# A graph layer's second pass: TensorE's results staged by ScalarE two experts ahead of VectorE, with the order fixed on four engines

## The chip, the cores and the metric

The kernel runs on one core of a Trainium2 chip. Its time is the device time of one execution in microseconds; the times of a kernel are given as the median of several runs. Engines are named as in the profile: PE is TensorE (matrix products, with PEld its weight loads), DVE is VectorE, ACT is ScalarE, POOL is GpSimd, which here issues the indirect DMAs, and SP is SyncE.

## The reference

Two graph layers run over 3125 nodes with 256 features and 103125 edges sorted by destination. Only the second one matters here:

```
W   = einsum('rb,bio->rio', comp, basis)              # 8 relations
agg = segment_sum((xn @ W[r])[src, edge_type], dst)   # a sum over each node's edges
h   = layernorm(gelu(agg + xn @ loop_w + h_bias + xn))
x   = x + h + linear_attention(xn)
xn  = layernorm(x) ; logits = xn @ Wr + br            # 8 experts, the best 2 weighted by softmax
x   = x + sum_e w[:, e] * (gelu(xn @ W1[e] + b1[e]) @ W2[e] + b2[e])
```

Everything is float32. The kernel computes all eight experts for every node and multiplies by the weight, which is zero for six of them.

## The kernel before

The nodes lie in 25 tiles of 128, with 128 nodes on the partitions and 256 features behind one another; `x` (3.2 MB in SBUF) holds all tiles. The last tile, 24, is partly filled. The table of `h` is complete at about 1396 us of the profiled execution, and the second pass follows it; until about 1500 us the jobs beside its gathers are those of the attention. The pass has two things to do at once.

**Edges.** For each tile of nodes, the rows of a table of `h` in HBM are gathered, 128 rows at a time, one row for each node of the tile. A gather is one indirect DMA issued by POOL (L193, `gt<-htab_f,idx2g`). The gathers go into a pool of five buffers (`gp1`), each of which takes up to four. When the gathers of one buffer have landed, DVE adds the blocks up: a 128x512 add and a 128x256 add among the blocks (L1356), and a 128x256 add to the sum of the tile (L1361). This is called an add chain here. A buffer is free for POOL again when its chain is through.

**Groups.** The tiles are worked through in groups of 4, 2, 4, 3, 3, 2, 2, 2, 1, 1 and 1 tiles (15 to 18 first, then 23 and 24, then from 19 to 22 downwards). The first group's sums are begun while the table is still being written (L2114 adds those, one instruction for up to four tiles). When the sums of a group are complete, a list of jobs is put on a queue, `bg`, and these jobs are done between the add chains of the next group. After each chain the loop hands out credit, in proportion to the gathers of that chain (0.9 to 1.3 for each, by how much work is queued), and takes jobs off the queue, each with a cost written beside it, until the credit is used up. The jobs of a group of k tiles are:

- `sums_a`, `sums_b`, `sums_c`: the products of `loop_w` and of the attention's part for each tile (`loops`, L2300 to L2302, on PE into PSUM), then two DVE adds that read PSUM (`mg`, L2307, and `x`, L2308) and a Gelu into `hh` (L2309).
- `states_a` to `states_d`: the two layer norms, with square roots on ACT (`root`, L2327).
- `routes_a` and `routes_b`: transposes and logits on PE (L2370, L2378), and the routing weights `wf` on DVE, with an exponent on ACT (L214) in the middle (`top2`).
- `shares`: the transposed weights, and the product with the experts' output biases (`constants`, L2425).
- `step(0)` to `step(9)`: `hidden(e)` does 8 products for an expert (four blocks of 128 hidden features, two halves of the input, L2408) into four PSUM banks, each followed by a Gelu on ACT (L2412) into `hT`. `outputs(e)` does four products a tile into PSUM (L2439), two tiles to a bank, with two banks in turn. `take`, at the start of the next step, is DVE's: one instruction a tile, `x = py * w + x` (L2458), which reads the product in PSUM and `x` in SBUF; the bias's product is added by L2450.

The last four steps of a group are kept back (`late`) and put between the first jobs of the next group. When a group is finished its tiles are put on the list `leaving`, and are scattered to the output (L240, an indirect DMA on POOL) between later gathers; those of tiles below 11 leave after the last gather.

The order of the instructions on DVE and POOL is that of the program (`manual_schedule`); the order on PE and ACT is chosen by a scheduler. All engines run their queues in order and wait for one another by semaphores.

Of the kernel before, what the change touches and what calls it, by code (L numbers as in the profile page):

```python
# [20 lines left out]
P = 128  # L21
# [39 lines left out]
SECONDS = 5  # L61

# [38 lines left out]
def gps_kernel(ctx: ExitStack, tc: tile.TileContext, a, out):  # L101
# [1215 lines left out]

    def fast():
        fx = ExitStack()
# [245 lines left out]
        with ExitStack() as l0x:  # L1565
# [376 lines left out]
            ET = mybir.EngineType  # L1942
# [216 lines left out]
        with ExitStack() as l1x:  # L2159
# [23 lines left out]
            f1 = l1x.enter_context(tc.tile_pool(name="f1", bufs=3))  # L2183
# [57 lines left out]
            def att_ctx(t):  # L2241
                r = rows(t)
                pt = ps_tr.tile([P, 2, P], F32, name="pt")
                PE.transpose(pt[:r, 0, :], kT[:, t * P : t * P + r], ident)
                ks = kp.tile([P, P], F32, name="ks1", bufs=3)
                S.activation(ks[:r, :], pt[:r, 0, :], AF.Copy, scale=rs2[:r, t : t + 1])
                PE.matmul(pctx, ks[:r, :], x[:r, t, :], start=(t == 0), stop=(t == NT - 1))

            def att_sum():
                S.copy(g_t, pctx)  # L2250
# [35 lines left out]
            class Group:  # L2286


                def __init__(self, tiles, accs):
                    self.tiles, self.accs = tiles, accs  # L2290
                    self.k, self.s = len(tiles), slice(tiles[0], tiles[-1] + 1)
                    self.at0, self.n = tiles[0] * P, sum(rows(t) for t in tiles)
                    self.hT, self.ys = {}, []

                def loops(self, a, b):

                    for j in range(a, min(b, self.k)):
                        pa = self.pa[j] = ps_mm.tile([P, 512], F32, name="mm")
                        at = slice(self.tiles[j] * P, (self.tiles[j] + 1) * P)
                        PE.matmul(pa, xT[:, 0, at], w_lu[:, 0, :], start=True, stop=False)  # L2300
                        PE.matmul(pa[:, :D], ones_row, b_h, start=False, stop=False, skip_group_check=True)
                        PE.matmul(pa, xT[:, 1, at], w_lu[:, 1, :], start=False, stop=True)  # L2302

                def gelus(self, a, b):
                    for j in range(a, min(b, self.k)):
                        t, mg, pa = self.tiles[j], self.accs[j], self.pa.pop(j)
                        V.tensor_tensor(mg, mg, pa[:, :D], op=ALU.add)  # L2307
                        V.tensor_tensor(x[:, t, :], x[:, t, :], pa[:, D:], op=ALU.add)  # L2308
                        S.activation(self.hh[:, j, :], mg, AF.Gelu)  # L2309

                def sums_a(self):
                    self.hh = fin.tile([P, 4, D], F32, name="hh")
                    self.mvh = [small.tile([P, 4, 2], F32, name=f"mvh{i}") for i in range(2)]
                    self.rsh = [small.tile([P, 4], F32, name=f"rsh{i}") for i in range(3)]
                    self.pa = {}
                    self.loops(0, 2)

                def sums_b(self):
                    self.gelus(0, 2)
                    self.loops(2, 4)  # L2320

                def sums_c(self):
                    self.gelus(2, 4)
# [41 lines left out]
                def routes_a(self):  # L2365
# [9 lines left out]
                    self.pl = ps_tr.tile([P, 512], F32, name="pt")  # L2375
                    for j, t in enumerate(self.tiles):
                        for c in range(2):
                            PE.matmul(  # L2378
                                self.pl[:, j * NX : (j + 1) * NX], xT[:, c, t * P : (t + 1) * P], wr1[:, c, :],
                                start=(c == 0), stop=(c == 1),  # L2380
                            )

                def routes_b(self):
                    k = self.k
                    lg1 = fin.tile([P, 4, NX], F32, name="lg1")
                    V.tensor_tensor(
                        lg1[:, :k, :], self.pl[:, : k * NX].rearrange("p (j e) -> p j e", e=NX),
                        br1[:, None, :].to_broadcast([P, k, NX]), op=ALU.add,
                    )
                    w_full, _ = top2(lg1[:, :k, :], k, fin)  # L2390
                    V.tensor_copy(wf[:, self.s, :], w_full)

                def shares(self):
# [6 lines left out]
                    self.constants()  # L2400

                def hidden(self, e):
                    n, at0 = self.n, self.at0
                    hT = self.hT[e] = f1.tile([P, FC, 4 * P], F32, name="hT1")
                    for f in range(FC):
                        ph = ps_mm.tile([P, 512], F32, name="mm")
                        for c in range(2):
                            PE.matmul(  # L2408
                                ph[:, :n], w1s[e][:, c, f * P : (f + 1) * P], xT[:, c, at0 : at0 + n],
                                start=(c == 0), stop=(c == 1),  # L2410
                            )
                        S.activation(hT[:, f, :n], ph[:, :n], AF.Gelu, bias=b1[:, e, f : f + 1])  # L2412

                def bank(self):
                    turn[0] += 1
                    return ps_acc.tile([P, 512], F32, name="py", tag=f"acc{1 + turn[0] % 2}")

                def constants(self):

                    for j0 in range(0, self.k, 2):  # L2420
                        pb = self.bank()
                        two = self.tiles[j0 : j0 + 2]
                        for j, t in enumerate(two):
                            r, at = rows(t), (j0 + j) * P
                            PE.matmul(  # L2425
                                pb[:r, j * D : (j + 1) * D], self.wT[:, at : at + r], b2a, start=True, stop=True
                            )
                        self.ys.append((None, two, pb))

                def outputs(self, e):  # L2430

                    hT = self.hT.pop(e)
                    for j0 in range(0, self.k, 2):
                        py = self.bank()
                        two = self.tiles[j0 : j0 + 2]
                        for j, t in enumerate(two):
                            r, at = rows(t), (j0 + j) * P
                            for f in range(FC):
                                PE.matmul(  # L2439
                                    py[:r, j * D : (j + 1) * D], hT[:, f, at : at + r], w2s[e][:, f, :],  # L2440
                                    start=(f == 0), stop=(f == FC - 1),
                                )
                        self.ys.append((e, two, py))

                def take(self):

                    for e, two, py in self.ys:
                        if e is None and rows(two[-1]) == P:
                            d = x[:, two[0] : two[-1] + 1, :].rearrange("p t d -> p (t d)")
                            V.tensor_tensor(d, d, py[:, : len(two) * D], op=ALU.add)  # L2450
                            continue
                        for j, t in enumerate(two):
                            r = rows(t)
                            d, y = x[:r, t, :], py[:r, j * D : (j + 1) * D]
                            if e is None:
                                V.tensor_tensor(d, d, y, op=ALU.add)
                            else:
# [202 lines left out]
```

## Time and profile before

| What | us |
|---|---|
| median of 7 runs | 2478.44 |
| lowest to highest of them | 2476.69 to 2487.56 |
| the profiled execution, its own time | 2480.69 |
| its span | 2478.9 |

| Engine, whole span | busy us | share |
|---|---|---|
| POOL | 1723.6 | 70% |
| PE | 1695.7 | 68% |
| DVE | 1267.0 | 51% |
| ACT | 560.6 | 23% |

A row of instruction groups reads: line, engine, operation, output <- input, shape, count, then busy time in us, the mean of one in ns, and the idle time of the engine just before these instructions with what ended most of it. "issue" means that the engine waited for nothing that the profile shows. In a row of the timeline the first number is the start, the second the duration, and the brackets hold the idle time before it and its releaser. In a table of windows each engine has its busy time and, in parentheses, its instructions.

### The profile page before, as it was taken

What the parts mean: (1) busy time and instruction counts of PE and PEld (TensorE: products, weight loads), DVE (VectorE), ACT (ScalarE), POOL (GpSimd) and SP (SyncE); (2) the same over time, 40 slices, a digit from 0 to 9 for tenths busy, and PEclk for the clock granted to TensorE, in tenths of its full rate; (3) what the DMA queues carried; (4) which work ended last, traced back from release to release, by engine and by line L of the source; (5) the groups of instructions that cost most, each with busy time, mean ns of one, the idle gap of its engine ahead of it and who ended that gap; (6) DMA issues with size and microseconds to landing.
All of it is one profiled execution on the core that took longest, in us unless ns stands there. A gap on an engine that the chain in (4) does not pass through costs nothing.

```text
span 2478.9 us, 20996 instructions
## 1 busy us (share of the span) xinstructions
PE 1695.7 (68%) x6033; PEld 1106.6 (45%) x6033; DVE 1267.0 (51%) x3537; ACT 560.6 (23%) x1275; POOL 1723.6 (70%) x1830
## 2 busy tenths in 40 slices
PE   3446777403926614375799736997889799797987
PEld 2323444202614302243444323665556567575876
DVE  7654556436544545444656335464536365454552
ACT  4222321001201101021322122131213132232333
POOL 4577777777777777777016776777777777777771
PEclk9777887655967766777799967998899899888988
DMA  6544444344344443444146834333333333333330
GB/s 192 141 110 110 108 107 127 105 105 140 103 105 107 107 106 104 107 105 105 61 181 231 289 112 136 103 107 111 98 107 105 105 102 103 103 103 103 102 101 23
DMA packets 125962, 290.09 MB, mean 117 GB/s; under 512 B 41386, under 2 KB 63982, under 8 KB 122632
## 3 DMA queue, kind: packets, MB, share of 16 engines
q0 software_dynamic: 83184, 230.02, 33.9%
q1 hardware_dynamic: 38122, 55.88, 6.6%
q10 hardware_dynamic: 4526, 2.71, 0.4%
q8 instruction: 51, 0.84, 0.1%
q14 instruction: 79, 0.65, 0.1%
HBM read 249.07 MB, written 39.41 MB: 116 GB/s over the span
## 4 chain that ended last, share of the span: by engine, by line
PE 19%; POOL 12%; issue 9%; DVE 5%; DMA 4%; ACT 1%; DVEq 0%; POOLq 0%; ACTq 0%
POOL gt L193 12%; PE mm L2408 6%; PE py L2439 6%; PE mm L188 5%; DMA gt<-htab_f,idx2g 3%; DVE gt L1356 1%; DMA out_dram<-x,id_i 1%; DVE bnst L162 1%; PE pt L2378 1%; DVE acc L1361 0%; DVE x L2458 0%; DMA gt<-htab_f,soon 0%; PE mm L2302 0%; DVE x L2343 0%; PE mm L2300 0%
## 5 line engine op out<-in xcount | busy, mean ns | idle before, releaser
L193 POOL DMA_INDIRECT gt<-btab,idx x814 | 799.9, 983 | 253.1 <-issue 223.6
L193 POOL DMA_INDIRECT gt<-htab_f,idx2g x742 | 731.3, 986 | 236.5 <-issue 200.4
L1356 DVE TENSOR_TENSOR gt<-gt 128x256 f32<-128x256 f32 (+1 forms) x767 | 411.5, 537 | 228.0 <-DMA gt<-htab_f,idx2g 211.6
L2408 PE MATMUL mm<-xT,w 128*128 128x256 f32 (+4 forms) x1408 | 386.9, 429 | 61.6 <-DVE x L2308 59.8
L2439 PE MATMUL py<-w,hT 128*128 128x256 f32 (+1 forms) x1600 | 374.8, 389 | 17.6 <-DVE x L2458 17.4
L2439 PEld LDWEIGHTS py<-w,hT 128*128 128x128 f32 (+1 forms) x1600 | 305.8, 194 | 79.6 <-DVE x L2458 11.2
L2408 PEld LDWEIGHTS mm<-xT,w 128*128 128x128 f32 x1408 | 250.3, 203 | 173.8 <-issue 128.7
L1620 DVE COPY slots<-gt 128x4 f32<-128x4 f32 (+1 forms) x214 | 38.5, 180 | 436.2 <-DMA gt<-btab,idx 436.0
L2412 ACT ACTIVATE hT<-mm,b 128x256 f32<-128x256 f32 (+4 forms) x352 | 170.7, 495 | 377.1 <-PE mm L2408 373.2
L188 PE MATMUL pt<-w_own,xT 128*128 128x256 f32 x100 | 39.5, 531 | 250.3 <-DVE acc L1845 250.3
L188 PE MATMUL mm<-w_rel,xT 128*128 128x512 f32 x400 | 176.1, 598 | 3.0 <-ACT xT L183 2.9
L1361 DVE TENSOR_TENSOR acc<-acc,gt 128x256 f32<-128x256 f32 x371 | 158.5, 427 | 12.7
L2458 DVE SCALAR_TENSOR_TENSOR x<-py,wf,x 128x256 f32<-128x256 f32 x200 | 87.8, 477 | 146.5 <-PE py L2439 146.3
L188 PEld LDWEIGHTS pt<-w_own,xT 128*128 128x128 f32 x100 | 24.3, 268 | 261.3 <-DVE acc L1845 254.8
L188 PEld LDWEIGHTS mm<-w_rel,xT 128*128 128x128 f32 x400 | 75.4, 191 | 96.1 <-issue 84.3
L1503 PE MATMUL mm<-xT,w 128*128 128x384 f32 (+2 forms) x320 | 94.6, 460 | 14.3 <-DMA w<-in_f_W_dram 14.3
L1863 PE MATMUL pmean<-ones,xt 128*128 128x1 f32 (+1 forms) x100 | 21.9, 323 | 119.9 <-DVE xt L171 119.9
L193 POOL DMA_INDIRECT gt<-htab_f,soon x72 | 75.8, 1053 | 39.0 <-issue 18.9
L1852 ACT ACTIVATE rs<-rs 128x3 f32<-128x3 f32 (+2 forms) x11 | 2.2, 203 | 434.6 <-DVE rs L1851 434.6
L1532 PE MATMUL mm<-w,hT 128*128 128x256 f32 x400 | 98.5, 401 | 2.0 <-ACT hT L1524 2.0
L1532 PEld LDWEIGHTS mm<-w,hT 128*128 128x128 f32 x400 | 77.0, 198 | 33.6 <-issue 18.9
L188 PE MATMUL mm<-w_qkv,xT 128*128 128x512 f32 (+1 forms) x200 | 88.8, 561 | 0.5 <-ACT xT L183 0.5
(436 smaller groups left out, 2111.8 us busy)
## 6 DMA issues: line engine op xcount, KB each, us to landing
htab_f<-hs SPq DMA_DIRECT2D x25, 1024.0 KB, 4.8
gt<-btab,idx POOLq DMA_INDIRECT x814, 2.8
gt<-htab_f,idx2g POOLq DMA_INDIRECT x742, 2.8
w<-in_f_W_dram SPq DMA_DIRECT2D x20, 512.0 KB, 8.8
ntab<-x SPq DMA_DIRECT2D x5, 640.0 KB, 10.9
btab<-bs SPq DMA_DIRECT2D x5, 640.0 KB, 3.8
x<-in_x_dram SPq DMA_DIRECT2D x4, 640.0 KB, 21.3
otab<-xn SPq DMA_DIRECT2D x16, 128.0 KB
```

What stands on the lines that cost most here:

```text
L162: V.bn_stats(out=st, in_=src)
L188: PE.matmul(ps, lhs[:, c, t * P : (t + 1) * P], w[:, c, :], start=start and c == 0, stop=stop and c == 1)
L193: G.indirect_dma_start(out=dst, out_offset=None, in_=table, in_offset=bass.IndirectOffsetOnAxis(ap=idx, axis=0))
L1356: V.tensor_tensor(gt[:, :h, :], gt[:, :h, :], gt[:, m - h : m, :], op=op)
L1361: V.tensor_tensor(acc, own(t) if i == 0 else acc, gt[:, 0, :], op=op)
L1503: PE.matmul(ph[:, :n], w1[:, i, c, f * P : (f + 1) * P], xT[:, c, at0 : at0 + n], start=(c == 0), stop=(c == 1),)
L1532: PE.matmul(py[:, i * D : (i + 1) * D], hTs[i][:, f, j * P : (j + 1) * P], w2[:, i, f, :], start=False, stop=(f == FC - 1), skip_group_che ...
L1620: V.tensor_copy(slots_of[t][:, U - 1 - k1 : U - 1 - k0], gw[:, : k1 - k0, D])
L2408: PE.matmul(ph[:, :n], w1s[e][:, c, f * P : (f + 1) * P], xT[:, c, at0 : at0 + n], start=(c == 0), stop=(c == 1),)
L2412: S.activation(hT[:, f, :n], ph[:, :n], AF.Gelu, bias=b1[:, e, f : f + 1])
L2439: PE.matmul(py[:r, j * D : (j + 1) * D], hT[:, f, at : at + r], w2s[e][:, f, :], start=(f == 0), stop=(f == FC - 1),)
L2458: V.scalar_tensor_tensor(d, y, wf[:r, t, e : e + 1], d, op0=ALU.mult, op1=ALU.add)
```

## The change

ScalarE takes TensorE's results out of PSUM, and DVE reads only SBUF. `loops` of a group is done ahead of its sums and copied into `hu`; `sums` adds from there, `x` with one instruction for the group. The logits are copied to `lg`. An expert's outputs are multiplied by the weight on the way out of PSUM (`brought`, one activation a tile, into one of two buffers `ys`), and DVE adds a buffer to `x` when it is two experts old (`taken`, one instruction for all tiles of the group). `behind` makes ScalarE's reads of an expert's banks wait for the last product of that expert. A step is now `hidden(i)`, `outputs(i - 1)`, `gelus(i)`, `brought(i - 1)`, with the biases' product in the place of expert -1, and it begins after `shares`. The last steps of a group (`hidden(6)` and on) stand between the first jobs of the next group, in three portions; for the last group they are the end of its own list. The order is fixed on PE and ACT too, and `hT` has two buffers instead of three. The attention's product for a tile (`att_add`) comes one tile later. Most removed lines are those of the functions printed above, and are left out here:

```diff
+YS = 2
...
+    def behind(ins, pe):
+        tc.add_manual_dep(
+            ins.ins, pe.ins.name, mybir.DependencyInfo(mybir.DependencyClass.Sync, mybir.DependencyReason.DATA),
+            reason="one signal for a row of products",
+        )
...
-            f1 = l1x.enter_context(tc.tile_pool(name="f1", bufs=3))
+            f1 = l1x.enter_context(tc.tile_pool(name="f1", bufs=2))
...
+                if t:
+                    att_add(t - 1)
+            kss = {}
+            def att_add(t):
+                r = rows(t)
+                PE.matmul(pctx, kss.pop(t)[:r, :], x[:r, t, :], start=(t == 0), stop=(t == NT - 1))
             def att_sum():
+                att_add(NT - 1)
...
-                    self.hT, self.ys = {}, []
...
+                    self.hT, self.ph, self.py = {}, {}, {}
+                def loops(self):
+                    self.hu = fin.tile([P, 4, 2, D], F32, name="hu")
+                    self.hh = self.hu[:, :, 0, :]
+                    pas = []
+                    for j, t in enumerate(self.tiles):
+                        pa = ps_mm.tile([P, 512], F32, name="mm")
+                        at = slice(t * P, (t + 1) * P)
                         PE.matmul(pa, xT[:, 0, at], w_lu[:, 0, :], start=True, stop=False)
                         PE.matmul(pa[:, :D], ones_row, b_h, start=False, stop=False, skip_group_check=True)
-                        PE.matmul(pa, xT[:, 1, at], w_lu[:, 1, :], start=False, stop=True)
...
+                        pas.append((pa, PE.matmul(pa, xT[:, 1, at], w_lu[:, 1, :], start=False, stop=True)))
+                    for j, (pa, _) in enumerate(pas):
+                        got = S.copy(self.hu[:, j, :, :], pa.rearrange("p (m d) -> p m d", m=2))
+                        behind(got, pas[-1][1])
+                def sums(self):
+                    k = self.k
                     self.mvh = [small.tile([P, 4, 2], F32, name=f"mvh{i}") for i in range(2)]
                     self.rsh = [small.tile([P, 4], F32, name=f"rsh{i}") for i in range(3)]
-                    self.pa = {}
...
+                    for j, mg in enumerate(self.accs):
+                        V.tensor_tensor(self.hh[:, j, :], self.hh[:, j, :], mg, op=ALU.add)
+                        S.activation(self.hh[:, j, :], self.hh[:, j, :], AF.Gelu)
+                    V.tensor_tensor(x[:, self.s, :], x[:, self.s, :], self.hu[:, :k, 1, :], op=ALU.add)
...
+                    self.lg = fin.tile([P, 4, NX], F32, name="lg1")
+                    S.copy(self.lg[:, :k, :], pl[:, : k * NX].rearrange("p (j e) -> p j e", e=NX))
                 def routes_b(self):
                     k = self.k
...
+                    lg = self.lg[:, :k, :]
+                    V.tensor_tensor(lg, lg, br1[:, None, :].to_broadcast([P, k, NX]), op=ALU.add)
...
+                def hidden(self, e):
+                    n, at0 = self.n, self.at0
...
+                        phs.append((ph, end))
+                def gelus(self, e):
+                    phs = self.ph.pop(e)
+                    hT = self.hT[e] = f1.tile([P, FC, 4 * P], F32, name="hT1")
+                    for f, (ph, _) in enumerate(phs):
+                        got = S.activation(hT[:, f, : self.n], ph[:, : self.n], AF.Gelu, bias=b1[:, e, f : f + 1])
+                        behind(got, phs[-1][1])
+                def outputs(self, e):
+                    hT = self.hT.pop(e) if e is not None else None
+                    self.py[e] = pys = []
+                    for j, t in enumerate(self.tiles):
+                        r, at = rows(t), j * P
+                        if j % 2 == 0:
+                            bank = self.bank()
+                        py = bank[:r, j % 2 * D : (j % 2 + 1) * D]
+                        if e is None:
+                            end = PE.matmul(py, self.wT[:, at : at + r], b2a, start=True, stop=True)
+                        for f in range(FC if e is not None else 0):
+                            end = PE.matmul(
+                                py, hT[:, f, at : at + r], w2s[e][:, f, :], start=(f == 0), stop=(f == FC - 1)
+                            )
+                        pys.append((py, end))
+                def brought(self, e):
+                    if len(brought) == YS:
+                        taken()
+                    ys = fin.tile([P, 4, D], F32, name="ys", bufs=YS)
+                    pys = self.py.pop(e)
+                    for j, (py, _) in enumerate(pys):
+                        t = self.tiles[j]
+                        r = rows(t)
+                        if e is None:
+                            got = S.copy(ys[:r, j, :], py)
+                        else:
+                            got = S.activation(ys[:r, j, :], py, AF.Copy, scale=wf[:r, t, e : e + 1])
+                        behind(got, pys[-1][1])
+                    brought.append((self, e, ys))
                 def shares(self):
...
-                    self.constants()
...
                 def step(self, i):
-                    self.take()
...
+                    self.hidden(i)
+                    self.outputs(i - 1 if i else None)
+                    self.gelus(i)
+                    self.brought(i - 1 if i else None)
+            brought = deque()
+            def taken():
+                group, e, ys = brought.popleft()
+                tiles = group.tiles
+                k = group.k - (tiles[-1] == NT - 1)
+                if k:
+                    d = x[:, tiles[0] : tiles[0] + k, :]
+                    V.tensor_tensor(d, d, ys[:, :k, :], op=ALU.add)
+                if k < group.k:
+                    d = x[:LAST, NT - 1, :]
+                    V.tensor_tensor(d, d, ys[:LAST, k, :], op=ALU.add)
+                if e == NX - 1:
+                    leaving.extend((tick[0] + 9, t) for t in tiles)
+            def all_of(*jobs):
+                return lambda: [job() for job in jobs]
+            def group_jobs(new, old):
+                k, c = new.k, old.k if old else 0
+                out = [(3.0, new.sums)]
+                if old:
+                    out.append((1.5 * c, all_of(
+                        lambda: old.hidden(6), lambda: old.gelus(6), lambda: old.outputs(5), lambda: old.hidden(7),
+                    )))
+                out += [(1.5, new.states_a), (1.5, new.states_b), (1.0, new.states_c)]
+                if old:
+                    out.append((2.0 * c, all_of(
+                        lambda: old.brought(5), lambda: old.gelus(7), lambda: old.outputs(6),
+                    )))
+                out += [(1.0, new.states_d), (4.0, new.routes_a)]
+                if old:
+                    out.append((2.5 * c, all_of(
+                        lambda: old.brought(6), lambda: old.outputs(7), lambda: old.brought(7),
+                    )))
+                out += [(2.0, new.routes_b), (2.0, new.shares)]
+                out += [((1.6 if i == 0 else 3.1) * k, lambda i=i: new.step(i)) for i in range(6)]
+                return out
+            def last_jobs(old):
+                c = old.k
+                return [
+                    (3.1 * c, all_of(
+                        lambda: old.hidden(6), lambda: old.gelus(6), lambda: old.outputs(5), lambda: old.hidden(7),
+                        lambda: old.brought(5), lambda: old.gelus(7), lambda: old.outputs(6), lambda: old.brought(6),
+                        lambda: old.outputs(7), lambda: old.brought(7),
+                    )),
+                    (1.0, lambda: [taken() for _ in range(len(brought))]),
+                ]
...
-            late = []
+            groups1 = [Group(EARLY, None)]
+            bg.append((2.0, groups1[0].loops))
             def after1(g, tiles, accs):
-                first, rest = Group(tiles, accs).jobs()
...
+                groups1[g].accs = accs
+                jobs = group_jobs(groups1[g], groups1[g - 1] if g else None)
+                if g + 1 < len(GROUPS1):
+                    groups1.append(Group(GROUPS1[g + 1], None))
+                    jobs.insert(len(jobs) - 2, (2.0, groups1[g + 1].loops))
+                else:
+                    jobs += last_jobs(groups1[g])
+                bg.extend(jobs)
...
                         credit -= cost
                 after1(0, EARLY, [sums[:, e, :] for e in range(len(EARLY))])
-            with tc.manual_schedule(engines={mybir.EngineType.DVE, mybir.EngineType.Pool}):
+            with tc.manual_schedule(engines={ET.DVE, ET.Pool, ET.PE, ET.Activation}):
...
```

## The prediction, made before the changed kernel ran

> **What bounds the kernel now.** The first view is the groups of instructions from 1500 to 2420 us, which is most of the second pass:
>
> ```profile
> L193 POOL DMA_INDIRECT gt<-htab_f,idx2g x683 | 669.3, 980 | 218.5 <-issue 183.7 <-DVE acc L1361 16.5 <-DVE gt L1356 3.4
> ...
> L1356 DVE TENSOR_TENSOR gt<-gt 128x512 f32<-128x512 f32 (+1 forms) x360 | 192.5, 535 | 217.0 <-DMA gt<-htab_f,idx2g 207.4 <-issue 3.0
> L2412 ACT ACTIVATE hT<-mm,b 128x256 f32<-128x256 f32 (+4 forms) x312 | 156.3, 512 | 356.2 <-PE mm L2408 353.6
> L2458 DVE SCALAR_TENSOR_TENSOR x<-py,wf,x 128x256 f32<-128x256 f32 (+1 forms) x189 | 82.5, 477 | 120.5 <-PE py L2439 120.2
> ```
>
> POOL issues one gather after another, 0.98 us each with 0.30 us of issue between. Its waits in that stretch (engine, line, what it waited for, total, times, longest) show that nearly nothing else holds it:
>
> ```profile
> POOL gt L193 <- issue: 183.7, 603, 0.3
> POOL gt L193 <- DVE acc L1361: 16.5, 20, 7.5
> ```
>
> Twenty gathers wait for DVE, 18 of them for the usual 0.30. The other two are 7.54 at 1539.65 and 2.78 at 1547.12, 9.7 us beyond the issue gap, both behind the first group's routing. DVE stands 120.2 us for TensorE's outputs and 207.4 us for gathered rows, so it has slack, and the five gather buffers hold 20 gathers, about 25 us, before a late DVE stops POOL. So the pass is POOL's chain of gathers: DVE time saved is worth nothing, and anything that lengthens a gather is paid in full. The last gather starts at 2410.75; from there a tail of dependent work runs to 2478.9. The timeline (start, duration, engine) has the larger stall, and a row of the tail to which I come back:
>
> ```profile
> 1539.65 0.94 POOL L193 DMA_INDIRECT gt<-htab_f,idx2g  x1 [7.54 <-DVE acc L1361]
> ...
> 2434.12 3.48 PE L2408 MATMUL mm<-xT,w 128*128 128x128 f32 x16
> ```
>
> Third, the timeline shows what can lengthen a gather:
>
> ```profile
> 1371.42 1.22 DVE L2114 TENSOR_TENSOR sums<-sums,gt 128x1024 f32<-128x1024 f32 x1
> 1371.48 1.97 POOL L193 DMA_INDIRECT gt<-htab_f,soon  x1 [0.30 <-issue]
> ...
> 1407.61 1.23 DVE L2114 TENSOR_TENSOR sums<-sums,gt 128x1024 f32<-128x1024 f32 x1 [1.92 <-DMA gt<-htab_f,soon]
> 1407.73 1.92 POOL L193 DMA_INDIRECT gt<-htab_f,soon  x1 [0.30 <-issue]
> ```
> ```profile
> 1561.05 1.14 DVE L1356 TENSOR_TENSOR gt<-gt 128x512 f32<-128x512 f32 x2
> 1561.47 1.08 POOL L193 DMA_INDIRECT gt<-htab_f,idx2g  x1 [0.30 <-issue]
> ...
> 1567.48 0.87 DVE L2458 SCALAR_TENSOR_TENSOR x<-py,wf,x 128x256 f32<-128x256 f32 x2 [4.83 <-PE py L2439]
> 1567.86 0.94 POOL L193 DMA_INDIRECT gt<-htab_f,idx2g  x1 [0.30 <-issue]
> ```
>
> An undisturbed gather takes 0.945. One that starts while DVE adds two SBUF tensors takes longer, by about what is left of that add less 0.13 us: 1371.42 + 1.22 − 1371.48 − 0.13 = 1.03, and it took 1.97. L2458, which reads PSUM and SBUF, does nothing to it (0.94).
>
> **The change, part by part.**
>
> *The new adds (the main term).* L2458 (PSUM) gives way to `taken`, which adds the staged `ys` to `x`, both in SBUF, one instruction per expert and group of up to 128x1024. Its width is that of L2114. For an add of length L that falls at random in POOL's cycle of 1.25 us, the mean delay is (L − 0.19)²/2.5 (0.19 = the 0.13 plus 0.06, the least lead by which the add was seen to win). L is 1.22 for four tiles, 0.69 for two (L2450's row shows 0.69 too), 0.43 for one, and by interpolation 0.96 for three. That is 0.43, 0.10, 0.023 and 0.24 us. Each group has nine such adds: 18 × 0.43 + 18 × 0.24 + 27 × 0.10 + about 38 small ones × 0.023 (the last group's come after the gathers) = 7.7 + 4.3 + 2.7 + 0.9 = 15.6. `sums` reads staged `hu` instead of PSUM: eleven wide adds, 1.7, and 25 of one tile, 0.6. Together 18 us. The same formula gives 26 us for the pass's present two-SBUF adds, and the gathers show about 25 above 0.945, so the size is sound. Bounds: 10 if the adds mostly follow an add chain at a kind phase, 26 at an unkind one (a four-tile add just before a gather costs 1.03, as at 1371).
>
> The Trainium skill, "SBUF — State Buffer", Who interferes with whom, says that a DVE instruction with two SBUF inputs contends with a GpSimd instruction that reads SBUF, but infers that building a DMA's descriptors is spared. By that inference this term would be 0 and the sum about 2482; the rows at 1371 and 1407 speak against it.
>
> *What it takes off DVE.* About 200 L2458 at 0.48 us, and the 120.2 us of standing for TensorE. Hidden under POOL's gathers before and after: worth 0, except at the places below.
>
> *What it puts on ScalarE.* Some 225 copies of one tile (`brought`), priced as L2309's 0.42: 95 us, and 25 of two tiles (`hu`) at about 0.6: 15 us. ScalarE is busy 27 of 100 us in this stretch and its Gelus wait 353.6 us for TensorE, so it is hidden if the order keeps it off the path. Table loads stay near the present 48.
>
> *The new waits on ScalarE.* `behind` makes the first Gelu of an expert wait for its last product instead of its own, with `brought` of the expert before queued behind the four Gelus and TensorE's next `hidden` waiting for the banks. In the order of a step TensorE then has `outputs` to do: 6.9 us for four tiles against Gelus of some 2.4, 1.89 for one tile against 4 × 0.37 = 1.5. Covered, so 0; without that cover it would be up to 1.5 an expert on TensorE, where late work reaches POOL only through the cushion.
>
> *The first group's routing.* It holds POOL at 1539.65. `sums` now waits for all four tiles' products and the copies behind the last of them (TensorE is done at 1512.1, as now; copies to about 1515), where now three tiles are through by then. Walking the same steps (states, transposes, logits, their copy on ScalarE, exponent) with the durations now seen puts the routing weights at 1541.5 against 1537.8, and POOL's stall ends at about 1543.2 against 1539.65. The second stall (2.78, behind the adds L2450 that wait 4.66 for TensorE) goes, since `taken` waits for nothing. Net +1 (−8 if the weights come early, +5).
>
> *The second group's routing.* TensorE now takes expert 0 of the first group only after `shares`, at about 1542; now it begins at 1527.67. Some of that it made up by idling, so about 10 us late remain, and the last output of group one ends near 1664 (now 1652.97). In the fixed order ScalarE does the second group's exponent after `brought(6)`, `outputs(7)` and `brought(7)`. So the weights come near 1670 (now 1661), and DVE stands from about 1647 with add chains queued behind it: 23 us plus an add chain of 1.6, against a cushion of 25. What waits for it is POOL, when the buffers are full. I put 5 us here: nearest is the first group's own 9.7 us of stalls, and the other end is 0, for now it has none. Later groups have fewer tiles and TensorE idles 10 to 22 of 100 us there, so I add none.
>
> *The tail.* From the last add chain's end (2415.72): now the routing weights come at +23.1, since ScalarE reloads tables twice and L2307 waits 2.05 for TensorE; then the last group's experts, at 3.51 us a pair once warm (1.95 + 1.89 for parts, some at half clock), the last scatter at +52.9. In the new order `sums` needs no TensorE, and the weights come at +17 to +19. But experts 0 and 1 of the last group no longer run their hidden products before the weights: all eight now follow, 0.35 + 29.1 us, plus 1.7 to 3.4 at half clock (16 products took 3.48 in the row above, 1.95 when warm), then 1.4 for `brought`, `taken` and the scatter: +49.7 to +53.0. Net −2 (−6 to +2).
>
> The clock is the place of a rule as well. TensorE's rows between 2434 and 2445 run at about half rate after gaps of 2 to 3 us. The skill's "TensorE: Matmul & The Clock Gate", What's actually happening, says that an idle window of about 3.4 us halves the clock; by it the new tail, with gaps of that length during the routing, would pay a half-rate window too, near my upper end of 3.4.
>
> *Scatters, gathers.* Same number in the same places on POOL; the new `leaving` condition moves a scatter by one job at most. 0.
>
> **Sum.** Profiled execution 2480.69 (span 2478.9 and 1.8 around it) + 18 + 1 + 5 − 2 = 2502.7. The median of the seven runs is 2.25 below the profiled one, so 2500.4: I say 2500. About 0.2%, 5 us, is what a measurement can tell here.
>
> **Rivals.**
> - *Faster: the standing DVE was what stopped POOL.* If decoupling DVE lets the first weights through before about 1532 (7.5 us earlier than I walk), both stalls go, −9.7, the tail gives −4, the second stall does not arise, and if the adds land between gathers (under 5 us in all) the time is 2478.4 − 13.7 + 3 = 2468. It decides only where contention is under about 9 us. For it: both stalls end on DVE. Against: `sums` now starts later, and L2114 hits gathers plainly. Chance 0.12.
> - *Nothing moves.* POOL-bound, with adds that contend little and the small terms cancelling (10 − 8 + 0 − 2): 2474 to 2483. Chance 0.14.
> - *The fixed order bites at each group.* If the exponent behind `outputs(7)` also stops POOL at the third and fourth groups, at 5 to 10 us each as for the second: 2500 + 10 to 20, so 2515. For it, TensorE's busy time in the windows at 1600 and 2000 (window, length, PE busy, and so on):
>
> ```profile
> 1600.00:1700.00 100.00, 96.12 (x401) 66.29 (x399) 54.35 (x139) 27.77 (x51) 76.24 (x79) 1.00 0.37 106
> ...
> 2000.00:2100.00 100.00, 98.97 (x380) 70.99 (x380) 55.05 (x142) 29.27 (x48) 75.77 (x78) 0.98 0.35 103
> ```
>
>   Against: those groups hand out their work at a slower rate. Chance 0.18.
> - My forecast, 2484 to 2512: 0.56.
>
> The range must leave out at most 0.2: from 2474, at the edge of the case of no movement, to 2517, past the middle of the fixed order's. Faster 0.12, same 0.14, slower 0.74.
>
> **What would show it.** Right: the mean L193 in 1500 to 2411 rises from 980 to about 1005 ns (18 us over 683 to 700), with the gathers over 1.3 us standing beside `taken`; DVE's wait for TensorE's outputs is gone; POOL has one wait of 7 to 12 us near 1543 and one of a few us near 1670. Wrong: gathers beside `taken` at 0.95; POOL's waits for DVE over 25 us in all; weights of the last group later than 20 us after the last chain.

## The result, and the profile after

The changed kernel takes 2499.0 us (median of 18 runs, 2491.72 to 2504.28), the kernel before 2479.09 (43 runs, 2474.47 to 2487.84): a ratio of 1.0074, 95% interval [1.0065, 1.0083]. The change costs 18 us by the ratio and 20 by the medians, where the forecast added 22 and said 2500.

The profiled execution took 2495.15, with a span of 2493.4, and is one of the shorter ones: its 735th gather from the end starts 4.7 us earlier than in the profile of before, ahead of everything that the change touches. So stretches of the second pass are compared, not whole spans. The groups of instructions from 1500 to 2430 us, with L195 now POOL's gather, L1366 the chain's first adds, L2456 ScalarE's copy of an expert's outputs and L2484 VectorE's `taken`:

```profile
L195 POOL DMA_INDIRECT gt<-htab_f,idx2g x680 | 680.9, 1001 | 221.6 <-issue 185.5 <-DVE acc L1371 16.6 <-DVE gt L1366 3.0
...
L1366 DVE TENSOR_TENSOR gt<-gt 128x512 f32<-128x512 f32 (+1 forms) x358 | 191.3, 534 | 335.7 <-DMA gt<-htab_f,idx2g 329.4
L2420 ACT ACTIVATE hT<-mm,b 128x256 f32<-128x256 f32 (+4 forms) x308 | 133.5, 516 | 212.5 <-PE mm L2410 212.4
...
L2456 ACT ACTIVATE ys<-py,wf 128x256 f32<-128x256 f32 (+1 forms) x188 | 76.7, 472 | 181.9 <-PE py L2439 141.5 <-issue 19.1 <-DVE x L2484 11.7
L2484 DVE TENSOR_TENSOR x<-x,ys 128x512 f32<-128x512 f32 (+3 forms) x84 | 66.4, 790 | 40.7 <-ACT ys L2456 27.6 <-ACT ys L2454 12.1
```

VectorE did get free: it now waits 329 us for gathered rows instead of 207, and the 120 us of standing for the experts' outputs are gone. In part it stands for ScalarE instead: its waits for ScalarE in this stretch add up to 129 us, 27 before. What it got was worth nothing, as the gather tells: its mean went from 980 to 1001 ns. The timeline shows the cause:

```profile
1579.56 1.23 DVE L2484 TENSOR_TENSOR x<-x,ys 128x1024 f32<-128x1024 f32 x1 [5.50 <-ACT ys L2456]
1579.72 1.88 POOL L195 DMA_INDIRECT gt<-htab_f,idx2g  x1 [0.30 <-issue]
1581.90 0.95 POOL L195 DMA_INDIRECT gt<-htab_f,idx2g  x1 [0.30 <-DVE gt L1366]
```

The gather that started 0.16 us into a four-tile add took 1.88, the next one 0.95. By the rule of the prediction: 1579.56 + 1.23 − 1579.72 − 0.13 = 0.94 over 0.945. POOL's waits for VectorE from 1500 to 2430 are these:

```profile
POOL gt L195 <- issue: 185.5, 609, 0.3
POOL gt L195 <- DVE acc L1371: 16.6, 12, 9.6
```

From the records of the last 695 gathers (the expectations below say 700, and their 39.8 and 25.6 are of these) one can add up three things: what the gathers took beyond 0.946 each, POOL's waits beyond its usual gap of 0.305, and the time from the last gather's start to the end of the span (the tail). The first of these is called the gathers' excess below. This table is the measure of all that follows; e1 to e4 are explained below.

| kernel | gathers beyond 0.946 | POOL's waits | first of the 695 to the last | tail |
|---|---|---|---|---|
| before | 25.6 | 10.4 | 927.9 | 68.2 |
| changed | 39.8 | 14.5 | 946.1 | 68.2 |
| e1_tiles | 36.3 | 13.4 | 941.8 | 74.3 |
| e2_no_adds | 28.7 | 14.6 | 935.1 | 62.7 |
| e3_dummies | 44.5 | 8.8 | 945.1 | 68.0 |
| e4_order | 27.0 | 18.8 | 938.6 | 61.5 |

Changed less before: 14.2 + 4.1 + 0 = 18.3, and the two stretches and tails differ by 18.2. That is the 18 us of the ratio. When each longer gather is put down to the add that covered its start, the `taken` adds have 10.6 us of the 14.2, and `sums`' add of `hu` 2.8; the 128x512 and 128x256 adds among a chain's blocks (L1356, now L1366) have 20.1 before and 21.2 after.

### The profile page after: what moved, and what is told of

Same layout as the page of the kernel before. It is cut to its first block, busy times and chain, and to the rows that moved or that the text cites. A ratio compares the mean times of both kernels' runs of the same rounds, so it can differ in the third digit from the quotient of the medians.

```text
span 2493.4 us, 21193 instructions
## 1 busy us (share of the span) xinstructions
PE 1696.1 (68%) x6033; PEld 1109.8 (45%) x6033; DVE 1249.1 (50%) x3415; ACT 627.1 (25%) x1525; POOL 1740.2 (70%) x1830
## 4 chain that ended last, share of the span: by engine, by line
PE 22%; POOL 11%; issue 8%; DVE 5%; DMA 3%; ACT 3%; DVEq 0%; POOLq 0%; SPq 0%; ACTq 0%
POOL gt L195 11%; PE py L2439 7%; PE mm L2410 7%; PE mm L190 5%; DMA gt<-htab_f,idx2g 2%; DVE gt L1366 1%; DMA gt<-htab_f,soon 1%; DVE bnst L164 1%; DMA out_dram<-x,id_i 1%; PE pt L2389 1%; ACT ys L2456 1%; PE mm L2322 0%; DVE x L2354 0%; ACT L216 0%; PE mm L2320 0%
## 5 line engine op out<-in xcount | busy, mean ns | idle before, releaser
L195 POOL DMA_INDIRECT gt<-btab,idx x814 | 800.3, 983 | 252.7 <-issue 222.7
L195 POOL DMA_INDIRECT gt<-htab_f,idx2g x742 | 746.7, 1006 | 240.5 <-issue 203.5
L1366 DVE TENSOR_TENSOR gt<-gt 128x256 f32<-128x256 f32 (+1 forms) x767 | 411.3, 536 | 346.6 <-DMA gt<-htab_f,idx2g 333.5
L2439 PE MATMUL py<-w,hT 128*128 128x256 f32 (+1 forms) x1600 | 380.2, 394 | 17.1 <-ACT ys L2456 17.1
L2410 PE MATMUL mm<-xT,w 128*128 128x256 f32 (+4 forms) x1408 | 376.8, 424 | 15.1 <-ACT hT L2420 14.5
L2420 ACT ACTIVATE hT<-mm,b 128x256 f32<-128x256 f32 (+4 forms) x352 | 146.1, 498 | 226.1 <-PE mm L2410 226.0
L1371 DVE TENSOR_TENSOR acc<-acc,gt 128x256 f32<-128x256 f32 x371 | 158.8, 428 | 12.8
L2456 ACT ACTIVATE ys<-py,wf 128x256 f32<-128x256 f32 x200 | 82.4, 472 | 190.6 <-PE py L2439 149.3
L2484 DVE TENSOR_TENSOR x<-x,ys 128x256 f32<-128x256 f32 (+3 forms) x99 | 72.7, 734 | 68.0 <-ACT ys L2456 50.5
L195 POOL DMA_INDIRECT gt<-htab_f,soon x72 | 75.8, 1052 | 39.2 <-issue 17.7
## 6 DMA issues: line engine op xcount, KB each, us to landing
ntab<-x SPq DMA_DIRECT2D x5, 640.0 KB, 10.6
x<-in_x_dram SPq DMA_DIRECT2D x4, 640.0 KB, 19.1
```

Source lines behind the costliest of these rows:

```text
L195: G.indirect_dma_start(out=dst, out_offset=None, in_=table, in_offset=bass.IndirectOffsetOnAxis(ap=idx, axis=0))
L1366: V.tensor_tensor(gt[:, :h, :], gt[:, :h, :], gt[:, m - h : m, :], op=op)
L1371: V.tensor_tensor(acc, own(t) if i == 0 else acc, gt[:, 0, :], op=op)
L2410: end = PE.matmul(ph[:, :n], w1s[e][:, c, f * P : (f + 1) * P], xT[:, c, at0 : at0 + n], start=(c == 0), stop=(c == 1),)
L2420: got = S.activation(hT[:, f, : self.n], ph[:, : self.n], AF.Gelu, bias=b1[:, e, f : f + 1])
L2439: end = PE.matmul(py, hT[:, f, at : at + r], w2s[e][:, f, :], start=(f == 0), stop=(f == FC - 1))
```

## Experiments

Theory P: a gather that starts under an add of two SBUF tensors waits for the rest of it, and POOL's chain pays that in full. Theory O: the adds hide on VectorE, and the fixed order with its waits is the loss.

**e1_tiles: the adds in smaller pieces.**

```diff
-                    d = x[:, tiles[0] : tiles[0] + k, :]
-                    V.tensor_tensor(d, d, ys[:, :k, :], op=ALU.add)
+                for j in range(k):
+                    d = x[:, tiles[j], :]
+                    V.tensor_tensor(d, d, ys[:, j, :], op=ALU.add)
```

> Theory P (a gather that starts under a two-SBUF add waits for the rest of that add): one add of 128x256 leaves at most 0.43 - 0.13 = 0.30 us to wait, one of 128x1024 up to 1.1. Over the last 700 gathers the time beyond 0.946 each was 39.8 us in the changed kernel; it should fall to about 30, and the time by 10, to 2489. If the next add of a row takes over the port before the gather gets it, P gives no fall. Theory O (the loss is the fixed order and its waits; the adds hide on VectorE): no change from 2499 or 1 to 2 us more, since VectorE only does more instructions.

Measured: 2496.36, ratio to before 1.007 [1.0058, 1.0082], no clear gain. The gathers' excess fell by 3.5, the part under `taken` from 10.6 to 5.5; rows of four adds back to back cost 0.13 us each, where one add of four tiles cost 0.37. So a gather does get in between two adds, as P has it, but there was less to win than the 10 us that I had said. Of the 4.3 us that POOL's stretch became shorter, all was lost again: the tail grew by 6.1. TensorE's last 50 us did not start earlier. The timeline of e1_tiles, where the second last group's experts begin:

```profile
2407.09 0.38 PE L2464 MATMUL pt<-ident,wf 128*8 128x128 f32 x1 [3.08 <-DVE wf L2401]
2407.26 3.62 PE L2410 MATMUL mm<-xT,w 128*128 128x128 f32 x16
```

In the changed kernel this row stands at 2405.68, so TensorE was 1.4 us later while POOL was 4.4 us earlier. That points to TensorE's own chain near the end (routing weights, half clock, eight experts) as nearly as long as POOL's, so that a few us won on POOL would show only if it came sooner too; no run here shortens that chain to test it.

**e2_no_adds: the adds away.**

```diff
-                    V.tensor_tensor(d, d, ys[:, :k, :], op=ALU.add)
+                    if e is None:
+                        V.tensor_tensor(d, d, ys[:, :k, :], op=ALU.add)
...
```

> Left out: the adds of the eight experts' staged outputs to x (taken does only the biases' product), so the output lacks the experts; order, copies and products stay. Theory P: the gathers' time beyond 0.946 falls from 39.8 by 12 to 14 us to about 26, as before the change, and the kernel to 2485 to 2487. Theory O: 2499 within 2 us.

Measured: 2478.48, ratio 0.9998 [0.9988, 1.0008], and an excess of 28.7, lower by 11.1. The waits stay (14.6). The time fell by 19 us (the difference of the ratios) and not by 12 to 14; in the profiles the stretch is 11.0 shorter, and the tail is 5.5 shorter as well; that part is due to what was left out, since without the adds the last scatters leave before TensorE is done. What P says is the 11.1.

**e3_dummies: the adds alone, in the kernel before.**

```diff
...
+                    if self.ys:
+                        zk = dummy[:, : self.k, :]
+                        V.tensor_tensor(zk, zk, dummy[:, 4 : 4 + self.k, :], op=ALU.add)
                     for e, two, py in self.ys:
```

> The kernel before, with its own order and its adds from PSUM, and one more add of two SBUF tensors, of the group's width, at the place of every take (9 a group, on a scratch tile); hT has two buffers as in the changed kernel. Theory P: the gathers' time beyond 0.946 rises from 25.6 by 13 to 16 us, and the time from 2479 to about 2493. Theory O: VectorE has 120 us of idle time in those waits and the 70 us of adds hide there: 2479 to 2481.

Measured: 2496.55, ratio 1.0077 [1.0064, 1.009]: as slow as the changed kernel, with the order, the waits (8.8) and the tail (68.0) of before. The excess rose by 19.0, more than the 13 to 16 expected, and the time is over the 2493 given. Nothing depends on these adds, and VectorE had room for their 70 us. The groups and the timeline of e3_dummies:

```profile
L193 POOL DMA_INDIRECT gt<-htab_f,idx2g x681 | 686.6, 1008 | 216.3 <-issue 181.3 <-DVE acc L1361 13.4 <-DVE x L2463 4.6
L2451 DVE TENSOR_TENSOR dummy<-dummy 128x512 f32<-128x512 f32 (+3 forms) x86 | 69.5, 808 | 0.0
```
```profile
1571.03 1.22 DVE L2451 TENSOR_TENSOR dummy<-dummy 128x1024 f32<-128x1024 f32 x1
1571.32 1.75 POOL L193 DMA_INDIRECT gt<-htab_f,idx2g  x1 [0.30 <-DVE acc L1361]
1573.37 0.95 POOL L193 DMA_INDIRECT gt<-htab_f,idx2g  x1 [0.30 <-issue]
```

The gather after it takes 0.95; the one under the dummy takes 1.75 (the rule gives 0.80 more). Of the excess, 16.6 us lie under the dummies. That the adds hide, as O says, falls with this run.

**e4_order: the order alone, the adds from PSUM again.**

```diff
...
-            got = S.activation(ys[:r, j, :], py, AF.Copy, scale=wf[:r, t, e : e + 1])
...
+                for t, (py, _) in zip(tiles, ys):
+                    r = rows(t)
+                    d = x[:r, t, :]
...
+                        V.scalar_tensor_tensor(d, py, wf[:r, t, e : e + 1], d, op0=ALU.mult, op1=ALU.add)
```

> The changed kernel with its fixed order on four engines and its order of jobs, but VectorE takes each expert's outputs from PSUM itself, tile by tile, ahead of the next expert's outputs (no ys). Theory P: the gathers' time beyond 0.946 returns to 25 to 28; the waits of GpSimd for VectorE are those of the changed kernel (14.5) or up to 10 more, since VectorE waits for TensorE again: 2485 to 2495. Theory O: the order alone is the loss: 2497 or more.

Measured: 2481.35, ratio 1.0010 [1.0000, 1.0019]. The groups of e4_order have the gather and the takes as they were before, VectorE's standing included:

```profile
L195 POOL DMA_INDIRECT gt<-htab_f,idx2g x681 | 669.1, 982 | 226.4 <-issue 181.9 <-DVE acc L1371 20.9 <-DVE rsh L2371 4.4
...
L2477 DVE SCALAR_TENSOR_TENSOR x<-py,wf,x 128x256 f32<-128x256 f32 (+1 forms) x189 | 81.6, 475 | 113.2 <-PE py L2441 113.2
```

So the order is nearly neutral, and with that the other half of O falls too. The time lies below the 2485 to 2495 that P gave: POOL waits 8.4 us longer than before (most of it in the first group), but the tail is 6.7 shorter, as the last exponent ends 13.7 us after the last chain instead of 22.1. This kernel keeps the staging of `loops` and of the logits. What the staging of the experts' outputs does is the difference of the changed kernel to e4_order: gathers +12.8 (10.6 under `taken`, 3.5 more under the chains' adds, the rest less), waits −4.3, tail +6.7, together +15.2; the ratios differ by 0.0064, or 15.9 us. The tail is part of it because ScalarE's copies stand in its queue ahead of the last exponent.

**Eight runs on another chip.** The remaining kernels ran on a chip where the kernel before itself took 2967 (e5 to e8) and 3001 us (f1 to f4). POOL is not the bound there: engines stand for 10 us and more (up to 29 in the second pass of f1_chain) for something that the profile doesn't show ("remote"), and POOL then waits for VectorE. Three rows of ScalarE in f1_chain's timeline:

```profile
1919.49 1.39 ACT L2413 ACTIVATE hT<-mm,b 128x512 f32<-128x512 f32 x2 [13.02 <-remote]
...
2292.70 1.23 ACT L2372 ACTIVATE xT<-pt,betf,gamf 128x384 f32<-128x384 f32 x2 [18.29 <-remote]
2353.59 2.00 ACT L2413 ACTIVATE hT<-mm,b 128x384 f32<-128x384 f32 x4 [23.54 <-remote]
```

ScalarE is not alone in this: before 2354 VectorE stands for 28.94 us and TensorE for 13.44, and all three go on within 1 us. Where these pauses come from stays open. The kernel before took from 2922 to 2981 us in the first of these two rounds, so runs of one kernel scatter there by 2%, and half a percent between two kernels is little. The times of this part say nothing on the first chip; the durations of gathers do, since an undisturbed one takes 0.945 here too.

*e7_chain and f1_chain* are the kernel before with smaller chain adds, for the 20 us of excess under L1356:

```diff
-                            V.tensor_tensor(gt[:, :h, :], gt[:, :h, :], gt[:, m - h : m, :], op=op)
+                            for i2 in range(h):
+                                V.tensor_tensor(gt[:, i2, :], gt[:, i2, :], gt[:, m - h + i2, :], op=op)
```

> The kernel before with the 128x512 add of each chain done as two of 128x256, in both passes. Port theory: 25.6 us of gathers' time beyond 0.946 in the last 700 fall to 18 to 20, as much again in the first pass: 2465 to 2470. Rival: VectorE's chains become 0.2 us longer and hit more gathers, or the first pass is held by VectorE: 2479 to 2484.

> The kernel before with the 128x512 add of each chain done as two of 128x256, in both passes, on a chip whose gathers land as in the profiles of before and after. Port theory: an add of 128x256 leaves at most 0.30 us to wait, one of 128x512 0.56; the time beyond 0.946 falls from 28 to about 15 us over the last 742 gathers and from 30 to 17 in the first pass, and the kernel by 20 to 27, to 2452 to 2459. Rival: what gathers give back, VectorE's longer chains or TensorE in the tail take again: 2470 to 2479.

Measured: 1.0061 [1.0014, 1.0108] and 1.0068 [1.0034, 1.0102]. The gathers did become shorter, in both passes; the page of f1_chain has 969 and 971 ns where that of before has 983 and 986:

```profile
L193 POOL DMA_INDIRECT gt<-btab,idx x814 | 788.7, 969 | 514.7 <-issue 222.7
L193 POOL DMA_INDIRECT gt<-htab_f,idx2g x742 | 720.4, 971 | 520.4 <-DVE acc L1362 267.7
```

The excess under the chain adds is 8.5 in the last 695, where before has 20.1 on the first chip and f3_pace, with whole adds on this one, 19.1. That is about 11 us in each pass by these rows, and P holds; but where POOL waits 268 us for VectorE, shorter gathers buy nothing, and the kernel was 0.6% slower. What it would give on the first chip was not measured.

*e8_pace and f3_pace* (one and the same kernel) give the first group's jobs of e4_order higher costs:

```diff
+                if not old:
+                    out = list(zip((4.0, 4.0, 6.0, 3.0, 3.0, 12.0, 4.0, 2.0), (job for _, job in out)))
```

> The kernel with the order alone, and the first group's first jobs at higher costs (4, 4, 6, 3, 3, 12, 4, 2), so that more add chains come between them. If GpSimd's waits of 17 us between 1529 and 1572 come from chains queued behind those jobs, they fall to 3 to 6 and the time to 2468 to 2472, below both kernels. Rival: the later routing makes TensorE late, and the waits come back at the second group (1650) or in the tail: 2478 to 2483.

> The order alone with the first group's first jobs at higher costs (4, 4, 6, 3, 3, 12, 4, 2), so that more add chains come between them. If GpSimd's waits of 17 us between 1529 and 1572 come from chains queued behind those jobs, they fall to 3 to 6 and the time to 2468 to 2472, below both kernels. Rival: the later routing makes TensorE late, and the waits come back at the second group (1650) or in the tail: 2478 to 2483.

Measured: 0.9987 [0.9942, 1.0031] and 0.9952 [0.9917, 0.9986]. The second run is faster than before by a little, the first not; the waits in question can't be told apart from this chip's own.

*f2_best* has both edits on e4_order.

> The order alone (adds from PSUM), the first group's first jobs at higher costs, and the split chain adds: both gains in one kernel. Port theory with the pacing theory: f1_chain less another 5 to 10: 2445 to 2452. Rival: the pacing gives nothing: within 3 us of f1_chain.

Measured: 1.0053 [1.0011, 1.0095]: nothing of the sum on this chip.

*e5_routes and f4_routes* put `routes_b` ahead of the old group's last portion in the changed kernel; *e6_order_routes* does so in e4_order.

```diff
-                out += [(1.0, new.states_d), (4.0, new.routes_a)]
+                out += [(1.0, new.states_d), (4.0, new.routes_a), (2.0, new.routes_b)]
...
-                out += [(2.0, new.routes_b), (2.0, new.shares)]
+                out += [(2.0, new.shares)]
```

> The changed kernel with the new group's routes_b put ahead of the old group's brought(6), outputs(7), brought(7), so ScalarE does the exponent before them. If GpSimd's wait of 3.63 at 1643.8 comes from ScalarE's fixed order, it goes, and the weights of the last group come 3 us sooner: 2494 to 2496, the gathers' time beyond 0.946 staying at 40. If the order is not what makes it late (the products are), it stays at 3 to 4 and the time at 2499.

> The changed kernel with the new group's routes_b put ahead of the old group's brought(6), outputs(7), brought(7). If GpSimd's wait of 3.63 at 1643.8 comes from ScalarE's fixed order, it goes, and the last group's weights come 3 us sooner: 2494 to 2496. If the products are what makes it late, the wait stays at 3 to 4 and the time at 2499.

> The kernel with the order alone (adds from PSUM), with routes_b ahead in the same way. Order theory: the wait of 1.83 at 1646.8 goes and the tail of 61.5 loses 1 or 2: 2478 to 2480. Rival: VectorE now stands at the logits for TensorE with no other work queued before it, and the wait grows: 2482 to 2485.

Measured: 1.0359 [1.0271, 1.0447] and 1.0207 [1.0153, 1.0261], against 1.0027 [0.9989, 1.0064]. The question, POOL's wait at 1643.8, is not settled by them. They do show that with staging the kernel loses 2 to 3.6% on this chip and without it nothing: e6_order_routes is e5_routes with the staging of the experts' outputs undone, and e5_routes took 3040 to 3072 us where e6_order_routes took 2938 to 2971. Why is not shown. In f4_routes VectorE waits 272.8 us for `ys` that ScalarE writes, but in f1_chain, without staging, it stands for 252 us as well, for "remote".

## Why the prediction was right, step by step

The sum forecast 18 + 1 + 5 − 2 = 22 us; the profiles have 14.2 + 1.1 + 3.6 + 0, less 0.6 for a short wait of before that is gone: 18.3. The main term and its mechanism were right, and it carried three quarters of the loss; that the total came within a few us is partly luck, since the adds cost less than forecast and the tail gave nothing back.

**The new adds.** Predicted 18, measured 14.2. The mechanism is shown from both sides by e2_no_adds (11.1 less without them) and e3_dummies (19.0 more from dummies alone). The term that was mis-sized is the 15.6 for `taken`, which measured 10.6: four-tile adds cost 0.37 each and not 0.43, three-tile ones 0.12 and not 0.24, two-tile ones 0.06 and not 0.10. The rule for one gather was exact: with the starts as they were, it gives 10.7. What is left is where in POOL's cycle an add falls, for which the prediction took a random place. Of the 84 `taken` (L2484) in the stretch, 52 come straight behind a chain; but the dummies do so too and cost 0.56 for four tiles, 16.6 in all. So whether 10.6 is due to the place or to chance stays open. The adds of `hu` were 2.8 and not 1.7.

What decides is where the operands lie, and not the kind of instruction. In the six profiles of the first chip, 115 gathers begin under an add `sums<-sums,gt` (both operands in SBUF) of four tiles with at least 0.2 us of it left: they are 0.51 us late on average, as the rule says. The 78 that begin so under `x = py * w + x` and the 21 under the add `x<-x,mm`, each with one operand in PSUM, are late by less than 0.01, and 20 under the same kind of instruction as `x = py * w + x` with both tensors in SBUF (`hu<-hu,mvh,gam`) by 0.18.

The Trainium skill, "SBUF — State Buffer", Who interferes with whom, says that a two-SBUF add contends with a GpSimd instruction that reads SBUF, and infers that the building of descriptors is spared. The 1.75 beside 0.95 in e3_dummies decides against the inference for these indirect DMAs.

**VectorE's relief and ScalarE's copies.** VectorE's relief was worth nothing, as said. `taken` does wait for ScalarE, though (39.7 us in 13 waits), where I had it wait for nothing; POOL shows no wait for it. The copies do cost, at the second group and in the tail below.

**The first group's routing.** Predicted +1. POOL's waits there, beyond the usual 0.305, were 7.23 + 2.47 and are 1.58 + 9.27: +1.1. The longer one ends at 1539.60; gathers of that time start 3.8 us earlier than in the profile of before, so that is 1543.4 against the 1543.2 walked. The second went, as forecast; the wait of 1.58 at 1526.53, for a chain queued behind the first group's norms, is new and was not foreseen.

**The second group's routing.** Predicted +5 near 1670, from the exponent behind `brought(7)`. Measured 3.63, at 1643.82, and another cause. The timeline of the changed kernel:

```profile
1626.57 0.74 ACT L2333 ACTIVATE hu<-hu 128x256 f32<-128x256 f32 x2
1627.03 0.43 DVE L164 BATCH_NORM_STATS2 bnst<-hu 128x6 f32<-128x256 f32 x1 [6.39 <-ACT hu L2333]
...
1632.05 2.42 ACT L2420 ACTIVATE hT<-mm,b 128x512 f32<-128x512 f32 x4 [4.75 <-PE mm L2410]
1634.49 1.28 ACT L2338 ACT_TABLE_LOAD   x1
1635.78 0.20 ACT L2338 ACTIVATE rsh<-rsh 128x2 f32<-128x2 f32 x1
1636.02 0.17 DVE L2350 RECIPROCAL rsh<-rsh 128x2 f32<-128x2 f32 x1 [7.33 <-ACT rsh L2338]
...
1643.82 0.98 POOL L195 DMA_INDIRECT gt<-htab_f,idx2g  x1 [3.94 <-DVE acc L1371]
...
1667.83 0.18 DVE L219 TENSOR_TENSOR t_w<-t_w,t_sel 128x16 f32<-128x16 f32 x1 [10.67 <-ACT t_w L216]
```

In ScalarE's fixed order the new group's Gelu stands behind `brought`, and its square root behind the Gelus of expert 6, which `behind` holds until the last product. VectorE stands 6.39 and 7.33 us for them, with chains queued behind. In e4_order, with the same order and no copies, only the second of these remains (5.38 us), and POOL's wait is 1.83 at 1646.75: the square root's place is the order's doing, the Gelu's that of the copies.

The exponent did come late, as forecast: the last row shows VectorE standing 10.67 us for it, and the weights are there at 1668.8 (forecast 1670). But VectorE stood from 1657 on, not from about 1647, after it had done the chains of the first stall; so the buffers never ran out, and POOL's gathers from 1650 to 1668 all start 0.30 after the end of the one before. The step that failed is this standing of 23 us; that a stall of about the forecast size arose elsewhere is luck.

**The tail.** Predicted −2, measured 0 (68.16 and 68.19). The last group's weights came 21.2 us after the last chain, where I walked 17 to 19 and before has 23.1; later than 20 was one of the prediction's own signs of being wrong. From the weights to the last scatter it took 32.1 us, near the 32.7 to 34.0 walked. The rows that the walk of the weights had too short, and the hidden products behind them:

```profile
2444.72 3.58 PE L2439 MATMUL py<-w,hT 128*128 128x256 f32 x8
...
2448.83 1.28 ACT L216 ACT_TABLE_LOAD   x1
2450.12 0.21 ACT L216 ACTIVATE t_w<-t_w 128x8 f32<-128x8 f32 x1
...
2451.50 3.39 PE L2410 MATMUL mm<-xT,w 128*128 128x128 f32 x16
```

`outputs(7)` ran at half clock (3.58 for 8 products, 1.89 warm) with the exponent behind it, and the first hidden products too (3.39, 1.95 warm), both after gaps of 2 to 3 us on TensorE; the granted clock was 0.53 and 0.54 in these two stretches, and 1.00 from 2457.4 to 2462. The prediction's walk has half clock for the hidden products only, not for `outputs(7)`. e4_order, where no copy stands ahead of the last exponent, has the weights at 14.7 us.

**Rivals.** The faster one needed both stalls to go; the first became longer. Nothing moves: the adds contend by 10.6 us. The fixed order that bites at each group did so once, at the second; after 1650 no gather waits longer than the usual 0.3.

## What to carry to other kernels

When one engine's chain is the bound, ask of a change first what it does to that engine's own instructions, and only then what it frees on others: here 120 us of waiting removed from VectorE bought nothing, and the 66 us of `taken` put on it in the stretch cost POOL 10.6. If GpSimd issues indirect DMAs without a break, let one operand of VectorE's adds come from PSUM, as e4_order does (2481 against 2499), or keep adds of two SBUF tensors short; shorter adds made gathers shorter in e1_tiles and f1_chain, but no kernel here became clearly faster by them. Staging through a third engine with a fixed order can put that engine's short, urgent steps behind the staging copies: look at each Gelu, square root and exponent in the new queue.

## What the runs showed of the hardware that I had not expected

A gather waits under one add only: in e1_tiles four adds back to back, 1.44 us in all, delay the gathers by 0.13 us a row, and in the changed kernel one add of 1.22 us by 0.37, so the wait ends with the add that is running. And two chips ran the same program at 2478 and at 2967 to 3001 us; on the second, engines pause for 10 us and more where the profile names no instruction of this kernel as the cause.
